# Adding the local attention mask on VectorE, in the pass that finds the row maximum, instead of with a TensorE product

## The chip, the cores and the metric

The kernel runs on one core of one Trainium2 chip. Each core has five engines with queues of their own: TensorE (PE in the profile; its weight loads are listed apart as PEld), VectorE (DVE), ScalarE (ACT), GpSimd (POOL) and SyncE (SP), which here only issues DMA transfers. Matrix products are written to PSUM, a small memory[...]; everything else on the chip lives in SBUF. The metric is the time of one execution on the device in microseconds (us); lower is better.

## The reference

For four sequences of 1024 tokens with 512 features, the reference computes a layer norm, then an attention block and a small matrix product, and adds both to the input. The attention has 16 heads of width 128 and two parts with the same queries. The *sparse* part scores each query against one compressed entry for every 4 tokens, keeps the top 8 and takes a softmax over them. The *local* part scores each query against the keys of its own window of 128 tokens and of the window before, with a band mask:

```
rel = i + WIN - j                       # i: query in window, j: key in the two windows
band = (rel >= 0) & (rel <= WIN)
sl = einsum('bhcqd,bhckd->bhcqk', qc, kw) * scale
sl = where(mask, sl, -1e30)             # mask: band, and no keys before the sequence
pl = softmax(sl)
ctx_local = einsum('bhcqk,bhckd->bhcqd', pl, vw)
merged = (ctx_sparse + ctx_local) * 0.5 # then times Wo
```

The mask of the local part is what the change is about. The first window of a sequence has no window before it, so only 128 keys take part there; all other windows have 256.

## The kernel before

**Tiling.** A *chunk* is 128 tokens of one sequence (number t, 32 in all; c = t mod 8 is its place in the sequence). A *unit* is one pair of heads of one chunk (number n, 256 in all; u = n mod 8 is the pair). Units of one chunk follow each other, u from 0 to 7.

**Pipeline.** The loop at L746 writes the order of all work by hand, and each engine executes its own instructions in that order; the instructions of different engines meet through semaphores, which are inserted from the data that they share. Step s does for several units at once: `scores(s)` for both heads (PE), `keep_context(s-2)` (ACT), `weigh(s)` for both heads (DVE, ACT), `queries(s+2)` (PE), `settle(s)` (DVE), the squares for unit s+2 (ACT, POOL), `settle_window(s)` (ACT), `to_output(s-2)` (PE), `turn(s)` (DVE, then SP), `values_of(s+1)` (PE), `normalize(s+2)` (DVE, POOL), `values(s-1)` (PE), `fetch(s)` (SP), `turn_keys(s+2)` and `fetch_keys(s+2)` (DVE, then SP), and `keep_values(s+1)` (ACT). Between these, two coroutines are advanced a little: `chunk_prep` (layer norm and compressed entries for the chunk after next) and `chunk_eight` (the small product with rounded operands, L422 its last DVE step). In the step with u = 1, `to_output` finishes a chunk, and DVE adds the product to the input (L716).

**The round trip of the keys.** `normalize` scales and rotates the queries and keys of unit s+2; `turn_keys` transposes them in blocks of 32 on DVE (L478, L481) and writes them to a buffer in DRAM (L486); `fetch_keys` reads them back transposed into qT and lkT (L497, L498). Two steps later `scores` uses them. In the same way `turn` (L623) sends the probabilities to DRAM (L631) and `fetch` brings them back (L657). All these transfers are issued by SP in program order, so the keys of unit s+2 are queued behind the probabilities of unit s.

**Scores and their mask.** `scores` fills one PSUM bank per head, sc (two such buffers). Its columns are: 0 to 127 the keys of the window before (absent when c = 0), 128 to 255 those of the own window, and from 256 on (c+1)*32 compressed entries. `loc` names the first group (256 columns, or 128 when c = 0), `spa` the second. In the kernel before, PE writes a mask first, as a product of an identity matrix with the mask in bf16 (L540), and then adds the scores to it in PSUM (L542 for the window before, L549 for the own). The compressed entries come next (L552), and the causal mask of their last 32 columns is added as another product with the identity (L553). A product of fp32 operands is executed as two passes, each with its own weight load; it counts as two instructions in the profile. A bf16 product is one pass.

**The softmax's first step.** `weigh` takes the negated maximum of the local columns (L574, DVE), the top eight of the compressed ones (L575), their negated maximum (L577) and marks them (L578); then ACT exponentiates the local columns (L579, with their sum) and the compressed ones (L582) out of the same bank.

Of the kernel before, what the change touches and what calls it, by code (L numbers as in the profile page):

```python
# [15 lines left out]
AF = mybir.ActivationFunctionType  # L16
ALU = mybir.AluOpType
AX = mybir.AxisListType

P = 128  # L20
# [4 lines left out]
BLK = 32  # L25
# [5 lines left out]
TAKEN = 3e38  # L31
# [7 lines left out]
def kernel(  # L39
# [26 lines left out]
    nc = tc.nc  # L66
# [14 lines left out]
    def blocks(v):  # L81

        return v.rearrange("p (b i) -> p b i", i=BLK)
# [89 lines left out]
    ident_b = const.tile([P, P], BF16, name="ident_b")  # L173
# [4 lines left out]
    mask_b = const.tile([P, 2 * P + NE], BF16, name="mask_b")  # L178
# [249 lines left out]
    def place(n):  # L428

        return divmod(n, NU)  # L430
# [94 lines left out]
    def columns(n):  # L525
        t, _ = place(n)
        c = t % NCH
        lo = 0 if c else P
        m = (c + 1) * NE
        return c, m, ds(lo, 2 * P - lo), ds(2 * P, m)  # L530

    def scores(n, h):
        t, _ = place(n)
        c, m, loc, spa = columns(n)
        w = units[n]
        qT, lkT = w["qT"], w["lkT"]
        ckT, _ = entries[t // NCH]
        sc = psum.tile([P, 512], F32, tag="sc", name=f"sc_{n}_{h}")
        q = qT[:, :, h]
        nc.tensor.matmul(sc[:, loc], ident_b, mask_b[:, loc], start=True, stop=False)  # L540
        if c:
            nc.tensor.matmul(  # L542
                blocks(sc[:, 0:P]),
                q,
                units[n - NU]["lkT"][:, :, ds(h * BLK, BLK)],
                start=False,
                stop=False,
            )
        nc.tensor.matmul(  # L549
            blocks(sc[:, P : 2 * P]), q, lkT[:, :, ds(h * BLK, BLK)], start=False, stop=True  # L550
        )
        nc.tensor.matmul(sc[:, spa], q, ckT[:, 0:m], start=True, stop=False)  # L552
        nc.tensor.matmul(  # L553
            sc[:, ds(2 * P + m - NE, NE)],
            ident_b,
            mask_b[:, 2 * P : 2 * P + NE],
            start=False,
            stop=True,
        )
        heads[n, h] = {"sc": sc}  # L560

    def weigh(n, h):
        c, m, loc, spa = columns(n)
        w = heads[n, h]
        sc = w.pop("sc")
        top = work.tile([P, 8], F32, tag="top", name=f"top_{n}_{h}")
        neg = work.tile([P, 2], F32, tag="neg", name=f"neg_{n}_{h}")
        tot = work.tile([P, 2], F32, tag="tot", name=f"tot_{n}_{h}", bufs=3)
        taken = work.tile([P, 2 * P], BF16, tag="taken", name=f"taken_{n}_{h}")
        prob = probs[h]  # L570
        if n % (NU * NCH) == 0:

            nc.gpsimd.memset(prob[:, 2 * P + NE : 4 * P], 0.0)
        nc.vector.reduce_max(neg[:, 0:1], sc[:, loc], AX.X, negate=True)  # L574
        nc.vector.max(top, sc[:, spa])  # L575

        nc.vector.tensor_scalar(neg[:, 1:2], top[:, 0:1], -1.0, 1e29, ALU.mult, ALU.min)  # L577
        nc.vector.match_replace(taken[:, 0:m], top, sc[:, spa], TAKEN)  # L578
        nc.scalar.activation(  # L579
            prob[:, loc], sc[:, loc], AF.Exp, bias=neg[:, 0:1], accum_out=tot[:, 0:1]  # L580
        )
        nc.scalar.activation(prob[:, spa], sc[:, spa], AF.Exp, bias=neg[:, 1:2])  # L582
        w.update(tot=tot, taken=taken, prob=prob)
# [162 lines left out]
    for s in range(-2, NN + 2):  # L746
# [6 lines left out]
        if u == 3 and 0 <= t and t + 2 < NT:  # L753
            load_x(t + 2)

        for_unit(s, (scores, 0), (scores, 1))
        for_unit(s - 2, (keep_context,))
        for_unit(s, (weigh, 0), (weigh, 1))
        for_unit(s + 2, (queries,))
        for_unit(s, (settle, 0), (settle, 1))  # L760
# [86 lines left out]
```

## Time and profile before

| | |
|---|---|
| median of 3 runs | 2910.0 us (2906.97 to 2914.53) |
| the profiled execution | 2908.4 us, of which 2906.6 us from its first to its last instruction (the span) |
| busy, share of the span | PE 98%, DVE 77%, ACT 44%, POOL 28% |
| one unit, on average | 2906.6 / 256 = 11.4 us |
| L540, mask product | 448 of 128x256 at 271 ns and 64 of 128x128 at 220 ns, PE |
| L574, maximum | 448 over 256 columns at 404 ns and 64 over 128 columns at 271 ns, DVE |

PE's passes overlap in the profile: a pass is listed from the time when it enters the array to its modelled end, so that the mean duration is longer than the distance to the next one. What a pass costs PE is that distance. The chain of waits, which lists the pieces of work that ended last in order of time, gives it directly: each piece there lasts until the next begins. On DVE too, an instruction that waits for nothing may begin before the end of the one before it is listed.

### The profile page before, as it was taken

The numbers are of one execution on the slowest core, as the hardware profiler recorded it, in microseconds if no ns is written. First come the engines' busy times: TensorE is split into PE (matmuls) and PEld (weight loads), VectorE is DVE, ScalarE is ACT, GpSimd is POOL, SyncE is SP. The second block draws the span as 40 slices with busy tenths as digits, with TensorE's granted clock in tenths as the row PEclk, the third lists the DMA queues.
The fourth block names the chain that finished last, engine by engine and source line by source line (L and its number), as shares of the span: only waits on it lengthen the run. The fifth ranks groups of instructions, "written<-read, shape, count | busy, mean of one in ns | idle before, by whom it ended". The sixth has DMA issues, their size and how long they took to land.

```text
span 2906.6 us, 49295 instructions
## 1 busy us (share of the span) xinstructions
PE 2855.3 (98%) x13705; PEld 1899.8 (65%) x13705; DVE 2224.0 (77%) x8636; ACT 1291.5 (44%) x5059; POOL 815.1 (28%) x1126
## 2 busy tenths in 40 slices
PE   5999999999999999999999999999999999999998
PEld 3566666666666666766666666666666666666666
DVE  5777777878777777788877777787887777877776
ACT  2444444444444444444444444444444444444443
POOL 3422222222233222222222332222322323222221
PEclk8999999999999999999999999999999999999999
DMA  8544445554444445454444444554454444455444
GB/s 242 162 129 132 130 134 141 145 146 140 128 115 131 127 130 140 143 144 140 142 126 119 127 130 126 146 148 137 141 143 117 128 124 126 126 146 149 139 142 120
DMA packets 634825, 399.86 MB, mean 138 GB/s; under 512 B 315796, under 2 KB 591030, under 8 KB 634550
## 3 DMA queue, kind: packets, MB, share of 16 engines
q1 hardware_dynamic: 622560, 383.18, 47.2%
q10 hardware_dynamic: 11990, 13.53, 1.5%
q8 instruction: 109, 1.79, 0.3%
q14 instruction: 166, 1.36, 0.2%
HBM read 208.30 MB, written 188.22 MB: 136 GB/s over the span
## 4 chain that ended last, share of the span: by engine, by line
PE 93%; DMA 3%; DVE 1%; SPq 1%; issue 0%; ACT 0%; POOL 0%; ACTq 0%; DVEq 0%; POOLq 0%
PE qp L437 30%; PE op L707 15%; PE vp L506 14%; PE cp L674 13%; PE sc L552 5%; PE sc L549 4%; PE sc L542 4%; PE ep L371 2%; PE qp L438 2%; PE sc L540 2%; DMA lkT<-qk 1%; PE lp L329 1%; PE fp L417 1%; DMA qk<-thb 1%; PE xp L319 0%
## 5 line engine op out<-in xcount | busy, mean ns | idle before, releaser
L437 PE MATMUL qp<-wqk,xnT 128*128 128x512 f32 x2048 | 947.1, 605 | 0.2 <-DMA wqk<-in_L_attn_Wlk_dram 0.2
L437 PEld LDWEIGHTS qp<-wqk,xnT 128*128 128x128 f32 x2048 | 371.3, 191 | 381.2 <-issue 371.0
L579 ACT ACTIVATE prob<-sc,neg 128x256 f32<-128x256 f32 (+1 forms) x512 | 235.6, 460 | 649.8 <-DVE taken L578 639.3
L707 PE MATMUL op<-wo,cT 128*128 128x512 f32 x1024 | 494.4, 605 | 1.0 <-ACT cT L689 1.0
L506 PEld LDWEIGHTS vp<-wlv,xnT 128*128 128x128 f32 x2048 | 388.9, 190 | 161.2 <-issue 103.1
L506 PE MATMUL vp<-wlv,xnT 128*128 128x256 f32 x2048 | 484.0, 379 | 0.0
L623 DVE STREAM_TRANSPOSE probB<-prob 128x512 f32<-128x512 f32 (+2 forms) x510 | 288.7, 603 | 161.1 <-ACT prob L605 157.8
L273 ACT ACTIVATE junk<-qp 128x128 bf16<-128x128 f32 x1024 | 283.6, 277 | 236.5 <-PE qp L438 200.8
L267 POOL TENSOR_SCALAR r<-ss 128x4 f32<-128x4 f32 x256 | 49.8, 194 | 1093.5 <-ACT junk L273 1088.1
L518 ACT COPY lv<-vp 128x256 f32<-128x256 f32 x256 | 95.1, 372 | 537.3 <-PE cp L674 455.1
L286 POOL TENSOR_TENSOR rb<-th,cs 128x256 f32<-128x256 f32 x256 | 247.1, 965 | 286.8 <-DVE th L459 286.8
L459 DVE SCALAR_TENSOR_TENSOR th<-qp,r,norm_w 128x128 f32<-128x128 f32 x1024 | 283.1, 337 | 40.1 <-POOL r L268 40.1
L674 PE MATMUL cp<-probT,lv 128*128 128x128 f32 x1920 | 297.7, 275 | 5.8 <-DMA qk<-thb 3.1
L707 PEld LDWEIGHTS op<-wo,cT 128*128 128x128 f32 x1024 | 181.7, 189 | 174.3 <-issue 96.6
L674 PEld LDWEIGHTS cp<-probT,lv 128*128 128x128 f32 x1920 | 274.8, 191 | 21.1 <-issue 3.6
L268 POOL TENSOR_TENSOR r<-r,nhalf 128x4 f32<-128x4 f32 x256 | 259.7, 1014 | 21.3
L674 PE MATMUL cp<-probT,cv 128*128 128x128 f32 x1536 | 255.2, 275 | 0.0
L574 DVE TENSOR_REDUCE neg<-sc 128x1 f32<-128x256 f32 (+1 forms) x512 | 198.3, 387 | 52.8 <-PE sc L553 52.8
L549 PE MATMUL sc<-lkT,qT 128*128 128x128 f32 x1024 | 210.6, 288 | 27.3 <-DMA lkT<-qk 27.1
L552 PE MATMUL sc<-ckT,qT 128*128 128x96 f32 (+7 forms) x1024 | 226.9, 303 | 0.0
L605 ACT ACTIVATE prob<-prob,tot 128x256 f32<-128x256 f32 (+1 forms) x512 | 222.6, 483 | 3.6 <-DVE tot L599 3.6
L674 PEld LDWEIGHTS cp<-probT,cv 128*128 128x128 f32 x1536 | 212.7, 192 | 0.0
(121 smaller groups left out, 4073.5 us busy)
## 6 DMA issues: line engine op xcount, KB each, us to landing
qk<-thb SPq DMA_DIRECT2D x1024, 64.0 KB, 2.0
pr<-probB SPq DMA_DIRECT2D x127, 512.0 KB, 2.6
probT<-pr SPq DMA_DIRECT2D x508, 128.0 KB, 2.9
pr<-probB SPq DMA_DIRECT2D x96, 384.0 KB, 2.3
probT<-pr SPq DMA_DIRECT2D x384, 96.0 KB, 2.4
qT<-qk SPq DMA_DIRECT2D x256, 128.0 KB, 2.3
lkT<-qk SPq DMA_DIRECT2D x256, 128.0 KB, 2.5
x<-_attn_hidden_states_dram SPq DMA_DIRECT2D x32, 256.0 KB, 3.1
```

The lines of the kernel that those rows point to most:

```text
L268: nc.gpsimd.tensor_tensor(r, r, nhalf[: ss.shape[0], 0:n], ALU.pow)
L273: nc.scalar.activation(junk[: src.shape[0]], src, AF.Square, accum_out=acc)
L286: nc.gpsimd.tensor_tensor(bb, x12, wide(cs[:, HALF:ROPE]), ALU.mult)
L437: nc.tensor.matmul(qp, xnT[:, k, :], wqk_sb[u][:, k, :], start=(k == 0), stop=False)
L459: nc.vector.scalar_tensor_tensor(th[:, i, :], qp[:, ts(i, D)], r[:, i : i + 1], norm_w[:, i // 2, :], ALU.mult, ALU.mult,)
L506: nc.tensor.matmul(vp[:, 0:256], xnT[:, k, :], wlv_sb[u][:, k, :], start=(k == 0), stop=(k == KK - 1),)
L549: nc.tensor.matmul(blocks(sc[:, P : 2 * P]), q, lkT[:, :, ds(h * BLK, BLK)], start=False, stop=True)
L552: nc.tensor.matmul(sc[:, spa], q, ckT[:, 0:m], start=True, stop=False)
L579: nc.scalar.activation(prob[:, loc], sc[:, loc], AF.Exp, bias=neg[:, 0:1], accum_out=tot[:, 0:1])
L623: nc.vector.transpose(pb[:, :, ds(h * g, g), :], prob[:, parts[0] * P : (parts[-1] + 1) * P].rearrange("p (g b i) -> p b g i", b=NB, i=BLK),)
L674: nc.tensor.matmul(blocks(cp[:, h, :]), v, probT[:, :, h * len(parts) + i - parts[0], :], start=(i == parts[0]), stop=(i == parts[-1]),)
L707: nc.tensor.matmul(op, cT[:, h, :], wo_sb[u][:, h, :], start=(u == 0 and h == 0), stop=(u == NU - 1 and h == 1),)
```

## The change

The mask product of the local columns is gone from `scores`; the first product into each group of columns now starts that group. In `weigh`, L574's maximum is replaced by one VectorE instruction that adds the mask to the local scores, multiplies by -1, writes the result back into the same columns of PSUM, and gives its minimum, which is the negated maximum of the masked scores. ACT's exponential then takes these columns with a factor of -1. The mask product of the compressed columns (L553) stays. The instruction issues two on DVE's queue: the pass itself and a read of the accumulator into neg; and as it writes sc, the next one on DVE, the top eight (L575 before), now waits for it.

```diff
         q = qT[:, :, h]
-        nc.tensor.matmul(sc[:, loc], ident_b, mask_b[:, loc], start=True, stop=False)
         if c:
             nc.tensor.matmul(
                 blocks(sc[:, 0:P]),
                 q,
                 units[n - NU]["lkT"][:, :, ds(h * BLK, BLK)],
-                start=False,
-                stop=False,
+                start=True,
+                stop=True,
             )
         nc.tensor.matmul(
-            blocks(sc[:, P : 2 * P]), q, lkT[:, :, ds(h * BLK, BLK)], start=False, stop=True
+            blocks(sc[:, P : 2 * P]), q, lkT[:, :, ds(h * BLK, BLK)], start=True, stop=True
         )
...
-        nc.vector.reduce_max(neg[:, 0:1], sc[:, loc], AX.X, negate=True)
+
+        nc.vector.tensor_tensor_reduce(
+            sc[:, loc], sc[:, loc], mask_b[:, loc], -1.0, TAKEN, ALU.add, ALU.min, neg[:, 0:1]
+        )
         nc.vector.max(top, sc[:, spa])
...
         nc.scalar.activation(
-            prob[:, loc], sc[:, loc], AF.Exp, bias=neg[:, 0:1], accum_out=tot[:, 0:1]
+            prob[:, loc],
+            sc[:, loc],
+            AF.Exp,
+            bias=neg[:, 0:1],
+            scale=-1.0,
+            accum_out=tot[:, 0:1],
         )
```

## The prediction

> **What bounds the kernel now.** I read the page's first and fourth part, then the chain of waits in order of time inside single units, then what DVE waits for inside one chunk, and last DVE's timeline.
>
> ```profile
> PE 2855.3 (98%) x13705; PEld 1899.8 (65%) x13705; DVE 2224.0 (77%) x8636; ACT 1291.5 (44%) x5059; POOL 815.1 (28%) x1126
> PE 93%; DMA 3%; DVE 1%; SPq 1%; issue 0%; ACT 0%; POOL 0%; ACTq 0%; DVEq 0%; POOLq 0%
> ```
>
> PE is 98% busy and carries 93% of the chain, so a pass taken from PE shortens the kernel if nothing else is late. How much a pass costs stands in the chain, in a unit with 256 local columns:
>
> ```profile
> 1559.99 0.11 PE cp L674
> 1560.11 0.11 PE sc L540
> 1560.21 0.24 PE sc L542 x2
> ...
> 1560.87 0.02 PE sc L553
> 1560.89 0.12 PE sc L540
> 1561.01 0.24 PE sc L542 x2
> ...
> 1561.66 0.02 PE sc L553
> 1561.67 3.53 PE qp L437 x8
> ...
> 1565.86 1.72 PE op L707 x4
> ```
>
> L540 takes 0.11 us for head 0 and 0.12 for head 1, though its row in the list of groups says 271 ns: 448 such products are 51 us, 64 shorter ones 4. But the last lines warn. Eight passes of L437 take 3.53 us where four equal passes of L707 take 1.72, so eight should take 3.44. The 0.09 us too many is the first weight load of L437: it stands behind L553, a 32-column product of 0.02 us, which is too short to hide it. After the change L542 of head 1 stands in just that place.
>
> In the chunks with c = 0 the mask product is half as long and hides only half a load:
>
> ```profile
> 820.08 0.02 PE sc L553
> 820.10 0.07 PE sc L540
> 820.16 0.29 PE sc L549 x2
> ```
>
> L549's two passes take 0.29 here and 0.23 to 0.24 behind a full pass.
>
> DVE is the other side. What it waits for in the last chunk of the second sequence, from 1385.1 to 1479.1 us (94.0 us, the widest scores, DVE's tightest stage):
>
> ```profile
> DVE th L288 <- POOL rb L286: 5.0, 8, 0.6
> DVE probB L623 <- ACT prob L605: 3.0, 3, 1.9
> DVE x L716 <- PE op L707: 2.8, 1, 2.8
> DVE neg L574 <- PE sc L553: 1.5, 2, 1.1
> DVE th L459 <- POOL r L268: 1.1, 2, 0.9
> DVE f L422 <- PE fp L417: 0.7, 1, 0.7
> ```
>
> The first line is inside DVE's own chain. The other five lead back to PE (L623 and L459 by way of ACT's squares, which wait for the queries): 9.1 us in eight units, DVE's spare time. The same five come to 12.8 us in the chunk from 848.0 to 934.3 us. DVE is thus behind PE, but not far from binding.
>
> The path by which a late DVE stops PE is the round trip of the keys. PE's largest wait is there:
>
> ```profile
> PE sc L549 <- DMA lkT<-qk: 27.1, 12, 9.1
> ```
>
> About 21 us of it are in the first 130 us. The others sit at one place: units 3 and 4 of a chunk, above all with c = 0. The keys of unit 3 leave DVE in unit 1 just behind L716, which had to wait for PE. In the other chunks these keys land up to about half a us before L549 needs them. So here there is hardly any slack, while the keys of most other units land 1 to 3 us early.
>
> **What the skill says.** The Trainium skill, "TensorE: Matmul & The Clock Gate", section on LDWEIGHTS, prices a load of 128 columns at 128/1.2 = 107 ns; the trace agrees, with 0.09 us exposed behind a product of 0.02 us. "VectorE: DVE Perf Modes", in the section on two Vector instructions with no wait between them, says that an operation which writes out its accumulator is two instructions; the trace shows it at L589, with a read of 82 ns. The same page's tier table puts a two-tensor operation with a PSUM operand at one element per cycle, and its errata section gives (N+151)/0.96 ns for an fp32 sum: an estimate of 424 ns for 256 columns. The trace has 688 ns at 512 columns (L716, one operand in PSUM), where that formula gives 691. No page prices a pass that writes PSUM, and no row of the trace shows one on DVE.
>
> **PE's part.** Head 0 of each unit: L542 follows a full pass of L674, which hides its load, so the whole L540 goes: 0.11 us. Head 1: L542 follows L553; of L540's 0.12 us, 0.09 comes back as exposed load: 0.03 us. That is 0.14 us for each of 224 units, 31 us. For the 32 units with c = 0: head 0 saves 0.06 (L540) and 0.05 (the load it half exposed), head 1 0.07 less 0.04 (0.09 exposed instead of 0.05): again 0.14, together 4.5. PE: 36 us less. The identity's weight loads under L540 (51 us of PEld) vanish with it; they already overlapped.
>
> **DVE's part.** I take the timeline of one unit:
>
> ```profile
> 1330.56 0.38 DVE L589 SCALAR_TENSOR_TENSOR prob<-taken,prob 128x224 f32<-128x224 bf16 x1
> 1330.86 0.08 DVE L589 DVE_READ_ACCUMULATOR prob<-taken,prob 128x1 f32 x1
> 1330.98 0.17 DVE L598 TENSOR_SCALAR tot<-tot 128x2 f32<-128x2 f32 x1
> ...
> 1341.93 0.41 DVE L574 TENSOR_REDUCE neg<-sc 128x1 f32<-128x256 f32 x1
> 1342.27 0.39 DVE L575 MAX8 top<-sc 128x8 f32<-128x224 f32 x1
> ```
>
> Now the maximum is followed by L575 after 0.34 us (0.31 to 0.34): L575 waits for nothing and starts under L574's tail. The new pass has the shape of L589: two streams, an accumulator, then an instruction that waits for it. There the distance from start to dependent start is 0.42 us at 224 columns; 32 more columns at 34 ns (420 against 386 ns in the rows) give 0.46. So +0.13 us per head, and the same at 128 columns (by the same distances there, 0.22 + 0.12 against 0.20): 512 x 0.13 = 67 us more on DVE, 0.26 us per unit. The bounds of the unknown: below, the pass cannot spare the read and the wait, 0.12; above, PSUM read and written in one bank at half rate adds 256 cycles' worth, 0.27 more, hence 0.40. I take 0.13, the nearest row.
>
> **The rest.** ACT's exponentials start 0.13 and 0.26 us later; ACT sits idle 650 us before them in all, and what is queued behind them, the squares, waits for the queries anyway (201 us). With that cover gone it would cost the same 0.26 per unit. The factor -1 is in the same instruction. POOL and SP issue nothing more or less; no DMA changes.
>
> **What comes back.** In a chunk with c > 0 DVE needs 16 x 0.13 = 2.1 us more and PE 1.1 less, 3.2 out of 9.1 to 12.8 us spare: PE stays the bound on average. But the key waits grow. Keys of unit 3: between the end of PE's output product in unit 1 and their use, DVE gains nothing (no `weigh` lies between), while PE arrives 0.14 + 0.11 = 0.25 us sooner; with slack between 0 and 0.5 I take 0.17 us, 28 chunks, 5 us. Keys of unit 4: one unit of DVE lies between (0.26) and PE comes 0.39 sooner; slack was mostly 0.5 to 2, so 0.1 us, 3 us. With c = 0 the waits at units 3 and 4 exist already: there DVE sets the pace from unit 1 to 4, and three chunks lose about 0.6 us each, 2 us. The start-up (units 0 to 4, DVE-paced) and the last units, where weighing lies on the final chain, cost two to four times 0.26 together: 2 us. In sum 12 us returned.
>
> 36 - 12 = 24 us: span 2906.6 to 2883, the profiled execution 2908.4 to 2884, and against the median of 2910.0, 2886 us. A measurement of this kernel tells about 0.3% (9 us) from no change.
>
> **Rivals.** *The full saving*: the loads hide after all (they might be fetched while L552 runs) and key waits don't grow: 51 + 4 = 55 us, 2855. L437 behind L553 speaks against it. *The wait takes the gain*: the new pass costs towards 0.40 per head. The keys of unit 4 then come 0.8 later on DVE's side with PE 0.4 sooner, so that a slack of 1 is gone, and those of unit 5 lose 1.6 and 0.5 of their 2 to 3. About 0.5 to 1 us per chunk more is lost, 16 to 32 us: 2902 to 2918, no change. L716's agreement with the price of plain streaming speaks against it. *VectorE becomes the bound, slower*: the pass has a large fixed cost, being of a kind that no row shows. With 9.1 to 12.8, on average about 10.7 us spare per chunk and 16 heads, DVE reaches today's period at 10.7/16 = 0.67 us more per head, so at 1.0 us from the pass to the top eight; each 0.1 us above costs 51 us, and at 1.1 us it is 2961.
>
> **Chances.** My forecast (2874 to 2896) 0.58; the full saving or near it (below 2874) 0.12; the eaten gain (2897 to 2918) 0.17, a sixth of it still over 0.3% faster; the slower case 0.13. Hence faster 0.73, same 0.14, slower 0.13. The range 2862 to 2916 holds the first case, half of the second and nearly all the third.
>
> **What would show it.** Right: L542's first pass takes about 0.20 us in head 1 and 0.12 in head 0; the new pass shows some 420 to 500 ns and an accumulator row of about 80 ns, the top eight starting 0.46 us after it; DVE's five PE-bound waits in the last chunk fall from 9.1 to about 6; lkT waits rise from 27 to 35 or 40 us. Wrong: the pass takes 0.7 us or more, PE's busy share falls visibly below 98% with lkT or qT waits spread over all units, or head 1 shows no exposed load.

## The result and the profile after

The changed kernel takes **2886.7 us** (median of four runs, 2879.2 to 2890.4) against 2911.0 us of the kernel before on the same chip (2907.0 to 2914.5). The ratio is 0.9914, with a 95% interval of 0.9890 to 0.9937: 24 us or 0.9% faster. The profiled execution took 2890.4 us with a span of 2888.6 us; it happens to be the slowest of the four, and where that matters a second profile of the same kernel stands beside it.

The names of the lines have moved by the edit. L541, L548, L551 and L552 are the old L542, L549, L552 and L553 (scores of the window before, of the own window, of the compressed entries, and their mask); L574 is the new pass, L577 the top eight (was L575), L612 ACT's scaling of the local probabilities (was L605), which stands behind the squares of unit s+2 (L273) in ACT's order, L630 and L723 the old L623 and L716, L681 the product with the probabilities (was L674).

The page's first part, busy time with its share of the span and the number of instructions:

```profile
PE 2828.1 (98%) x13193; PEld 1872.0 (65%) x13193; DVE 2298.1 (80%) x9148; ACT 1286.2 (45%) x5059; POOL 815.7 (28%) x1126
```

PE has lost its 512 mask products (13705 to 13193) and is still busy 98% of a shorter span. DVE has gained 512 instructions, the reads of the accumulator, and 74 us of busy time.

**What a unit saves on PE.** PE's timeline has this in a unit of the last chunk of the second sequence. Columns: start, listed duration, line, operation, tiles, operand shapes, count.

```profile
1387.89 0.40 PE L541 MATMUL sc<-lkT,qT 128*128 128x128 f32 x2
1388.13 0.40 PE L548 MATMUL sc<-lkT,qT 128*128 128x128 f32 x2
1388.36 0.60 PE L551 MATMUL sc<-ckT,qT 128*128 128x256 f32 x2
1388.80 0.18 PE L552 MATMUL sc<-mask_b,ident_b 128*128 128x32 bf16 x1
1388.83 0.48 PE L541 MATMUL sc<-lkT,qT 128*128 128x128 f32 x2
1389.15 0.40 PE L548 MATMUL sc<-lkT,qT 128*128 128x128 f32 x2
```

Read the distances from start to start. L541 of head 0 holds PE for 1388.13 - 1387.89 = 0.24 us, as before. L541 of head 1, which now stands behind the 32-column product L552, holds it for 1389.15 - 1388.83 = 0.32 us. The 0.08 us too many is, by the prediction's account, the weight load that nothing hides; experiment 6 tests that. The rows of the list of groups, with shapes kept apart, say the same. Before (busy time, mean ns of one, idle time ahead and what ended it):

```profile
L542 PE MATMUL sc<-lkT,qT 128*128 128x128 f32 x896 | 178.8, 281 | 1.1 <-DMA qT<-qk 1.1
```

The same row after:

```profile
L541 PE MATMUL sc<-lkT,qT 128*128 128x128 f32 x896 | 197.3, 302 | 3.3 <-DMA qT<-qk 2.1 <-ACT cT L696 1.0
```

A unit has four such passes. A mean that is 21 ns longer is one pass in four that is 0.08 us longer.

The distance from one unit's small mask products to the next unit's is the period of a unit. Unit by unit, after less before, its median is -0.136 us; 256 times that is 34.8 us. What is missing from 34.8 to the change of the span came back at single units. The table gives the excess over the median, in us, for both profiles of the changed kernel:

| | this profile | second profile | predicted |
|---|---|---|---|
| span, after less before | -18.0 | -24.8 | -24 |
| 256 x the median unit | -34.8 | -34.8 | -36 |
| first chunk of all and last chunk of all | +5.6 and +2.6 | +1.1 and +1.3 | +2 |
| other chunks with c = 0 | +1.9 | -1.0 | +2 |
| c > 0: from unit 2 to unit 3 | +4.7 | +4.3 | +5 |
| c > 0: from unit 3 to unit 4 | +0.4 | +2.3 | +3 |
| the rest | +1.7 | +2.0 | 0 |

Not all of this is waiting. In the first 130 us TensorE is granted only part of its clock, and not the same part in every execution. The rows give, for the 40 us from 40 to 80 us, PE's busy time, the granted clock as a share of full speed, the DMA share and GB/s: before, then this profile, then the second.

```profile
40.00:80.00 40.00, 30.20 (x127) 0.84 0.68 205
40.00:80.00 40.00, 28.06 (x96) 0.73 0.62 186
40.00:80.00 40.00, 30.77 (x120) 0.82 0.70 208
```

In this profile the clock is lower there, and the step from unit 1 to unit 2 alone is 3.1 us over the median; in the second profile, with nearly the clock of before, it is 0.6 us under it. This profile also has a stretch with a granted clock of 0.62 (1501.5 to 1506 us, in the first chunk of the third sequence, after a wait of 2.0 us for keys), and the unit there is 1.5 us over. So some 5 of its 16.8 us go with the clock (an estimate from these two places); the second profile's 10.0 us are the better measure of what the waits took. Over all executions on record the same shows: at a granted clock of 0.993, 0.994 and 0.995 the changed kernel has medians of 2889, 2884 and 2879 us (six, two and one executions), the kernel before 2913, 2911 and 2909 (six, 26 and 19), so that at like clock the gain is 24 to 30 us. Whether the change itself lowers the clock is not shown.

**What a head costs on DVE.** DVE's timeline of one head:

```profile
1344.18 0.40 DVE L574 CUSTOM_DVE_ANT_0 sc<-sc,mask_b 128x256 f32<-128x256 f32 x1
1344.50 0.14 DVE L574 DVE_READ_ACCUMULATOR2_ANT neg<- 128x1 f32 x1
1344.67 0.40 DVE L577 MAX8 top<-sc 128x8 f32<-128x224 f32 x1
```

From the pass to the top eight it is 0.49 us here; the median over the heads with 256 columns is 0.51, against 0.33 before. So a head costs DVE 0.18 us more, 92 us in all. The pass alone is only 10 ns longer than the maximum it replaces (414 ns against 404). What is new is the read of the accumulator, and that the top eight starts only after it:

```profile
L574 DVE CUSTOM_DVE_ANT_0 sc<-sc,mask_b 128x256 f32<-128x256 f32 x448 | 185.3, 414 | 10.8 <-PE sc L552 9.1
L574 DVE DVE_READ_ACCUMULATOR2_ANT neg<- 128x1 f32 x512 | 70.9, 138 | 0.0
```

**Who waits for whom.** The waits of DVE in the last chunk of the second sequence, 1375 to 1468 us (sum, count, longest):

```profile
DVE th L288 <- POOL rb L286: 5.0, 8, 0.6
DVE x L723 <- PE op L714: 2.2, 1, 2.2
DVE probB L630 <- ACT prob L612: 1.8, 3, 0.6
DVE th L459 <- POOL r L268: 1.4, 2, 1.1
```

Of the five waits that lead back to PE, two are gone, and the others come to 2.2 + 1.8 + 1.4 = 5.4 us where they were 9.1. PE's waits for the transfers, over the whole span:

```profile
PE sc L548 <- DMA lkT<-qk: 29.7, 12, 9.2
PE cp L681 <- DMA probT<-pr: 8.8, 4, 3.8
```

The keys' wait has grown by 2.6 us only (27.1 before), and the probabilities' by 6.2 (2.6 before).

### The profile page after: what moved, and what is told of

Read it like the earlier page. It is cut to its first block, busy times and chain, and to the rows that moved or that the text cites. A ratio compares the mean times of both kernels' runs of the same rounds, so it can differ in the third digit from the quotient of the medians.

```text
span 2888.6 us, 49258 instructions
## 1 busy us (share of the span) xinstructions
PE 2828.1 (98%) x13193; PEld 1872.0 (65%) x13193; DVE 2298.1 (80%) x9148; ACT 1286.2 (45%) x5059; POOL 815.7 (28%) x1126
## 5 line engine op out<-in xcount | busy, mean ns | idle before, releaser
L630 DVE STREAM_TRANSPOSE probB<-prob 128x512 f32<-128x512 f32 (+2 forms) x510 | 288.6, 603 | 99.1 <-ACT prob L612 96.2
L273 ACT ACTIVATE junk<-qp 128x128 bf16<-128x128 f32 x1024 | 284.2, 278 | 123.0 <-PE qp L438 95.7
L459 DVE SCALAR_TENSOR_TENSOR th<-qp,r,norm_w 128x128 f32<-128x128 f32 x1024 | 283.0, 337 | 53.6 <-POOL r L268 53.6
L681 PE MATMUL cp<-probT,lv 128*128 128x128 f32 x1920 | 298.2, 275 | 8.8 <-DMA probT<-pr 8.8
L681 PEld LDWEIGHTS cp<-probT,lv 128*128 128x128 f32 x1920 | 275.3, 192 | 24.2 <-issue 6.0
L681 PE MATMUL cp<-probT,cv 128*128 128x128 f32 x1536 | 255.6, 275 | 0.0
L548 PE MATMUL sc<-lkT,qT 128*128 128x128 f32 x1024 | 211.6, 289 | 30.1 <-DMA lkT<-qk 29.7
L551 PE MATMUL sc<-ckT,qT 128*128 128x96 f32 (+7 forms) x1024 | 226.9, 303 | 0.0
L612 ACT ACTIVATE prob<-prob,tot 128x256 f32<-128x256 f32 (+1 forms) x512 | 222.8, 484 | 2.8 <-DVE tot L606 2.8
L574 DVE CUSTOM_DVE_ANT_0 sc<-sc,mask_b 128x256 f32<-128x256 f32 (+1 forms) x512 | 203.4, 397 | 23.0 <-PE sc L552 21.2
L288 DVE TENSOR_TENSOR th<-thb,rb 128x128 f32<-128x128 f32 x256 | 87.2, 341 | 158.5 <-POOL rb L286 158.0
```

The costliest lines, as they stand in the source:

```text
L273: nc.scalar.activation(junk[: src.shape[0]], src, AF.Square, accum_out=acc)
L459: nc.vector.scalar_tensor_tensor(th[:, i, :], qp[:, ts(i, D)], r[:, i : i + 1], norm_w[:, i // 2, :], ALU.mult, ALU.mult,)
L548: nc.tensor.matmul(blocks(sc[:, P : 2 * P]), q, lkT[:, :, ds(h * BLK, BLK)], start=True, stop=True)
L630: nc.vector.transpose(pb[:, :, ds(h * g, g), :], prob[:, parts[0] * P : (parts[-1] + 1) * P].rearrange("p (g b i) -> p b g i", b=NB, i=BLK),)
L681: nc.tensor.matmul(blocks(cp[:, h, :]), v, probT[:, :, h * len(parts) + i - parts[0], :], start=(i == parts[0]), stop=(i == parts[-1]),)
```

## The experiments

Every time is a median, with its range, beside the kernel before on the same chip (2910.0 to 2911.1 us). "Per unit" is the median change of a unit's period against before. The local score columns are called loc, as in the code; lines marked ... leave out code.

**1. PE's part alone.** The local mask is left out altogether: no product, and the plain maximum. Against the changed kernel:

```diff
-        nc.vector.tensor_tensor_reduce(
-            sc[:, loc], sc[:, loc], mask_b[:, loc], -1.0, TAKEN, ALU.add, ALU.min, neg[:, 0:1]
-        )
+        nc.vector.reduce_max(neg[:, 0:1], sc[:, loc], AX.X, negate=True)
...
-            scale=-1.0,
```

> PE's part alone: the mask product of the local columns is taken out and nothing takes its place; VectorE finds the plain maximum as before. (The local scores are left unmasked.) My theory (head 0 saves 0.11 us, head 1 only 0.03, since the weight load of its first pass stands exposed behind the 32-column product): 35 us less PE time, some 4 us of it given back in waits for keys, so about 2879 us, and L437-like 0.20 us for the first pass in head 1. Rival (PE saves the whole 55 us and VectorE's dearer pass gives the other half back): about 2855 us.

Measured: 2880.0 us (2877.1 to 2882.9), ratio 0.9897 (0.9884 to 0.9910), per unit -0.136. So 31 us is what PE's part brings with no cost on DVE at all. The 55 us of the full saving do not exist in this order of work: the passes of L541 have a mean of 302 ns here too. The whole change stands at 2886.7, so DVE's part would cost some 7 us; the two intervals (0.9884 to 0.9910 and 0.9890 to 0.9937) overlap, so this is not told from nothing.

**2. DVE's part alone.** The mask product stays and the new pass is added; the mask is added twice.

```diff
-        nc.vector.reduce_max(neg[:, 0:1], sc[:, loc], AX.X, negate=True)
+        nc.vector.tensor_tensor_reduce(
+            sc[:, loc], sc[:, loc], mask_b[:, loc], -1.0, TAKEN, ALU.add, ALU.min, neg[:, 0:1]
+        )
...
-            prob[:, loc], sc[:, loc], AF.Exp, bias=neg[:, 0:1], accum_out=tot[:, 0:1]
+            prob[:, loc], sc[:, loc], AF.Exp, bias=neg[:, 0:1], scale=-1.0, accum_out=tot[:, 0:1]
```

> VectorE's part alone: the mask product stays on TensorE, and VectorE runs the new pass too (the mask is added twice, which changes nothing in the result). VectorE has 0.18 us more per head, 92 us in all. My theory: it is hidden except in waits for the keys of units 3 and 4 of a chunk, 2 to 8 us, so 2912 to 2918 us. Rival (VectorE's part costs what the change did not gain of 55 us): about 30 us more, 2940 us. If VectorE's time were on the path: 3000 us.

Measured: 2913.4 us (2908.1 to 2917.4), ratio 1.0011 (1.0004 to 1.0017), per unit 0.000. DVE does 92 us more work and the kernel takes 3 us longer. That is the cover at work: the five waits of DVE that the prediction counted as spare (the list of the kernel before is in experiment 4) fall from 389 to 302 us, by nearly as much as was added. Whether the same 92 us cost more when PE is faster at the same time (7 us by experiment 1) can't be told from these times.

**3. One head at a time.** Which head saves what? Both edits were made for one head only, `h == 0` or `h == 1`; the other keeps product and maximum. The edit for head 0:

```diff
+        product = h != 0
+        if product:
+            nc.tensor.matmul(sc[:, loc], ident_b, mask_b[:, loc], start=True, stop=False)
...
-                start=True,
-                stop=True,
+                start=not product,
+                stop=not product,
...
+        fused = h == 0
+        if fused:
+            nc.vector.tensor_tensor_reduce(
...
+        else:
+            nc.vector.reduce_max(neg[:, 0:1], sc[:, loc], AX.X, negate=True)
...
-            scale=-1.0,
+            scale=-1.0 if fused else 1.0,
```

> The change for head 0 of each unit alone; head 1 keeps the mask product and the plain maximum. My theory: head 0's product goes whole, 0.109 us x 256 = 28 us less PE time, VectorE has only half of its extra cost, some 4 us come back as waits: about 2886 us, as good as the whole change. Rival (both heads save the same, VectorE gives back in proportion): half of the change's gain, about 2899 us.

> The change for head 1 of each unit alone; head 0 keeps the mask product and the plain maximum. My theory: the exposed weight load takes 0.08 of the 0.11 us saved, 0.028 us x 256 = 7 us less PE time, some 3 us come back as waits: about 2906 us. Rival (both heads save the same): half of the change's gain, about 2899 us.

| | time, us | ratio | per unit | mean of the 896 L541 passes |
|---|---|---|---|---|
| head 0 | 2895.9 (2893.9 to 2897.6) | 0.9952 (0.9939 to 0.9965) | -0.109 | 282 ns |
| head 1 | 2906.6 (2902.4 to 2912.2) | 0.9991 (0.9983 to 0.9998) | -0.027 | 302 ns |

PE's saving splits just as the prediction had it, 0.11 and 0.03 us, and only head 1 shows the exposed load. The times are another matter. Head 1 fits. Head 0 was expected at 2886 and took ten more: of its 256 x 0.109 = 27.9 us, 13 came back, 8.0 of them on the way into unit 3, in steps of 1 to 2 us in a few chunks. The theory of this run (some 4 us of return) is wrong there. The two heads together gain 14.6 + 3.9 = 18.5 us, against 24 for the whole. Why head 0 alone lost more at unit 3 than the whole change does is left open.

**4. Where does DVE become the bound?** One or two plain maxima, whose result nobody uses, were added per head ahead of the new pass; the edit for one (`range(2)` for two):

```diff
+        for _ in range(1):
+            nc.vector.reduce_max(spare, sc[:, loc], AX.X, negate=True)
         nc.vector.tensor_tensor_reduce(
```

> The changed kernel with two plain maxima more per head on VectorE ahead of the new pass, results unused: 2 x 0.331 us by the distance measured before, so VectorE has 0.18 + 0.66 = 0.84 us per head more than in the kernel before. My theory (spare time of 9 to 13 us per chunk, used up at 0.67 us per head, each 0.1 us above costs 51 us): VectorE sets the pace, about 2911 + 87 = 2998 us, 2980 to 3020. Rival (VectorE is so loosely coupled that only the keys of units 3 and 4 come later): under 2930 us.

> The changed kernel with one plain maximum more per head, result unused: VectorE then has about 0.18 + 0.34 = 0.52 us per head more than in the kernel before. The run with two more stood at 0.97 us and lost 252 us, which with a slope of 512 heads puts the point where VectorE sets the pace of before at 0.97 - 0.49 = 0.48 us, not at the 0.67 of my prediction: the waits behind ScalarE and GpSimd (L623, L459) are no spare time of VectorE's, those behind TensorE alone are (97 + 53 + 41 us and a part of L623's 158). Theory now: 2910 + 0.04 x 512 = 2930 us, 2918 to 2945. The prediction's threshold: 2910 us or less.

| DVE per head against before | time, us | ratio | change |
|---|---|---|---|
| +0.18 us (the change) | 2886.7 | 0.9914 | -24 us |
| +0.52 us (one more) | 2960.7 (2955.5 to 2977.1) | 1.0182 (1.0156 to 1.0208) | +50 us |
| +0.97 us (two more) | 3162.0 (3159.0 to 3163.2) | 1.0862 (1.0847 to 1.0877) | +252 us |

DVE got 0.97 us more with two maxima, not the 0.84 expected: both write the same small tile, so the second waits for the first and starts 0.44 us after it, where one that waits for nothing starts after 0.33. Even so, both times came out far above what was expected; the expectation for one more maximum was already revised after the run with two, and is still 30 us too low. The prediction took 0.67 us per head as the point at which DVE reaches the period of the kernel before. With 0.52 the kernel should have been faster than before, or the same; it is 50 us slower. The page of the kernel with two more shows that PE no longer binds (211 of its PE records are missing from the trace, 12982 against 13193 weight loads, nearly all of them L438 at 0.21 us each, so that the true share is about 93%):

```profile
PE 2911.4 (92%) x12982; PEld 1914.6 (61%) x13193; DVE 2653.3 (84%) x10172; ACT 1238.6 (39%) x5059; POOL 814.6 (26%) x1126
```

But DVE is busy only 84%. What it still waits for says where the count of the spare time went wrong (DVE's waits over the whole span; sum, count, longest):

```profile
DVE th L288 <- POOL rb L286: 157.4, 255, 0.6
DVE probB L633 <- ACT prob L615: 93.0, 122, 4.2
DVE th L459 <- POOL r L268: 61.9, 83, 2.3
DVE spare L576 <- PE sc L552: 14.7, 5, 6.4
DVE x L726 <- PE op L717: 12.0, 5, 6.0
```

And the same view of the kernel before:

```profile
DVE probB L623 <- ACT prob L605: 157.8, 154, 4.6
DVE x L716 <- PE op L707: 97.4, 32, 6.1
DVE neg L574 <- PE sc L553: 52.8, 52, 6.0
DVE f L422 <- PE fp L417: 41.1, 31, 1.9
DVE th L459 <- POOL r L268: 40.1, 83, 2.3
```

The waits that name PE have nearly gone: the output product from 97 to 12 us, the scores from 53 to 15, L422 from 41 to less than one. But the wait for ACT's scaling (L605, L615 here), which stands behind the squares in ACT's order, falls from 158 to 93 only, and the one for POOL, which works on the squares' sums, rises from 40 to 62. The prediction traced these two back to PE, since the squares wait for the queries. With two more maxima that is over: ACT's idle time ahead of the squares, in the rows of before and of this kernel, falls from 236.5 to 37.8 us ("remote" is what the view prints where it can name no releaser).

```profile
L273 ACT ACTIVATE junk<-qp 128x128 bf16<-128x128 f32 x1024 | 283.6, 277 | 236.5 <-PE qp L438 200.8 <-POOL rb_e L286 7.1 <-POOL er L268 2.2
L273 ACT ACTIVATE junk<-qp 128x128 bf16<-128x128 f32 x1024 | 283.3, 277 | 37.8 <-remote 8.8
```

So 155 us of the two waits remain although the squares hardly wait for PE any longer: they were never spare in this order of work. What DVE could give is the difference of the two lists: 85 + 38 + 41 + 65 - 22 = 207 us, or 0.40 us per head, not 0.67. The curve agrees: if all DVE time past the threshold counts in full, 252 us from 512 heads put it at 0.97 - 0.49 = 0.48 us. It has no sharp corner. From +0.18 to +0.52 us per head the time rises by 74 us where 174 were added to DVE, from there to +0.97 by 201 where 230 were added. The loss begins before the average is used up. With one more maximum the median unit is still 0.135 us shorter than before, as in the change; the loss sits in single units, and shows on PE in part as small waits for queries and keys:

```profile
PE sc L548 <- DMA lkT<-qk: 41.3, 31, 9.0
PE sc L541 <- DMA qT<-qk: 18.8, 26, 1.7
```

These two are 28 us more than in the change (29.7 and 2.1), of the 74 us; the rest was not followed. A rival for the loss with two more is TensorE's clock, 0.98 over the whole span where before had 0.995. It is not the cause: two chunks of the same place in their sequence (c = 6), one with a granted clock of 1.00 and one with 0.98, both last 102.0 us, against 93.3 before.

**5. Is the SP queue what makes the keys late?** The keys of unit s+2 are written behind the probabilities of unit s in the same queue. Here the writes of the keys are issued ahead of the fetch of the probabilities. DVE's transposes move with them in the program, but the fetch has no work for DVE, so DVE's own order stays:

```diff
+        for_unit(s + 2, (turn_keys,))
         if s < NN - 1:
             for_unit(s, (fetch,))
...
-        for_unit(s + 2, (turn_keys,), (fetch_keys,))
+        for_unit(s + 2, (fetch_keys,))
```

> The changed kernel with the writes of the keys ahead of the fetch of the probabilities in SP's order; the reads of the keys stay behind it. The keys then leave some 0.5 us sooner, the probabilities land some 2 to 3 us later. If the keys' round trip through SP is what gave back the 10 us (my theory), the waits for lkT beyond the first 130 us (about 8 us in the profile) fall to 2 or less and the time to about 2880 us, provided the probabilities are still in time; if they are not, PE waits at the product with the values instead and the time goes up. Rival (the waits come from VectorE's pass itself): the same 2887 us.

Measured: 2892.4 us (2891.7 to 2896.2), ratio 0.9940 (0.9928 to 0.9953): 5.7 us above the change, though the two intervals touch. PE's waits:

```profile
PE cp L681 <- DMA probT<-pr: 24.6, 38, 4.5
PE sc L548 <- DMA lkT<-qk: 14.5, 5, 9.3
```

After the first 130 us the key waits are down to 1.3 us (7.0 in the change), as the theory of the queue says. But the probabilities are late in their place, 38 times instead of 4. The two round trips share one queue with no slack for either; putting one first moves the wait to the other.

**6. Is the exposed load due to what stands ahead of it?** If so, a long pass ahead of L541 of head 1 must hide it. The mask products of the compressed entries (L552) of both heads were moved behind the scores of both heads, into a function of their own:

```diff
-        nc.tensor.matmul(
-            sc[:, ds(2 * P + m - NE, NE)],
...
+    def end_scores(n):
+        _, m, _, _ = columns(n)
+        for h in range(2):
+            nc.tensor.matmul(
+                heads[n, h]["sc"][:, ds(2 * P + m - NE, NE)],
...
-        for_unit(s, (scores, 0), (scores, 1))
+        for_unit(s, (scores, 0), (scores, 1), (end_scores,))
```

> The changed kernel with the two 32-column mask products of the compressed entries put together behind both heads' other products. Head 1's first product then follows a pass of head 0 with as many columns as there are compressed entries (32 in the first chunk of a sequence, 256 in the last). My theory (a weight load[...] is hidden only as far as the pass before it lasts): the 0.08 us exposed in head 1 is gone in the last chunks (0.08 us per unit less), halved in the middle, unchanged in the first; about 9 us in all, 2878 us, if VectorE's later start on head 0 (by some 0.7 us) costs nothing. Rival (the 0.20 us of the first pass is not an exposed load): no unit gets shorter, 2887 us.

PE's timeline of this kernel; L557 holds the two mask products:

```profile
1380.59 0.60 PE L551 MATMUL sc<-ckT,qT 128*128 128x256 f32 x2
1381.03 0.39 PE L541 MATMUL sc<-lkT,qT 128*128 128x128 f32 x2
1381.26 0.40 PE L548 MATMUL sc<-lkT,qT 128*128 128x128 f32 x2
```

L541 of head 1 now holds PE for 0.23 us, and the mean of its passes is back:

```profile
L541 PE MATMUL sc<-lkT,qT 128*128 128x128 f32 x896 | 181.5, 284 | 6.6 <-DMA qT<-qk 3.8 <-ACT cT L700 2.6
```

The saving per unit grows with the length of the pass ahead, L551, which has 32 columns for c = 0, 64 for c = 1 and so on: -0.14, -0.17, -0.19, -0.22 us for c = 0 to 3, and -0.23 from c = 4 on. That is the exposed load, disappearing as the cover gets longer: L541 of head 1 holds PE for 0.29, 0.26 and 0.24 us at c = 1, 2 and 3 and 0.23 from c = 4 on, where the change has 0.32 throughout. Summed over the places in the sequence, PE's saving is 52 us. The kernel takes 2885.3 us (2879.5 to 2887.0), ratio 0.9910 (0.9892 to 0.9927): not to be told from the change. Its profile's span is 24 us shorter than before's, so that 28 of the 52 us came back, 5.7 of them on the way into unit 3 and most of the others spread over many units. Two causes offer themselves: with DVE 0.18 us per head slower, little cover is left to use a faster PE; and head 0's scores are complete only after head 1's, so that DVE starts on them later. Experiment 8 keeps the second and removes the first.

**7. What makes the pass dear on DVE?** The masked scores were written to SBUF, into prob, where ACT exponentiates them in place. The top eight then does not wait for the pass, which no longer writes the tile (sc, one bank of PSUM) that it reads.

```diff
-            sc[:, loc], sc[:, loc], mask_b[:, loc], -1.0, TAKEN, ALU.add, ALU.min, neg[:, 0:1]
+            prob[:, loc], sc[:, loc], mask_b[:, loc], -1.0, TAKEN, ALU.add, ALU.min, neg[:, 0:1]
...
             prob[:, loc],
-            sc[:, loc],
+            prob[:, loc],
             AF.Exp,
```

> The changed kernel with the masked scores written to SBUF, where the exponential then reads them, instead of back into PSUM. The top eight then need not wait for the pass. Expected: the pass itself 0.42 us as before if writing PSUM costs nothing extra, less if it does; from its start to the top eight 0.40 to 0.48 us instead of 0.51; the time within 5 us of 2887, since VectorE's time is hidden.

DVE's timeline:

```profile
1331.29 0.38 DVE L574 CUSTOM_DVE_ANT_0 prob<-sc,mask_b 128x256 f32<-128x256 f32 x1
1331.61 0.08 DVE L574 DVE_READ_ACCUMULATOR2_ANT neg<- 128x1 f32 x1
1331.61 0.39 DVE L577 MAX8 top<-sc 128x8 f32<-128x224 f32 x1
```

The top eight starts together with the read of the accumulator, 0.32 us after the pass (median 0.34, as before the change). So the 0.18 us per head lies in the order "pass, read, then the top eight", and not in the second operand or the multiplication: the pass takes 403 ns into SBUF, 414 into PSUM, and the plain maximum 404. Two parts of it can be told apart. A wait alone costs 0.11 us, as between the two useless maxima of experiment 4, which write to SBUF (0.44 us against 0.33). Most of the rest, 0.06, is the read, 138 ns in the change and 82 here. L589's read also takes 82 ns, although an instruction waits for it, and its pass writes SBUF; so the output in PSUM is the likelier reason for the longer read than the waiter. But L589 is another instruction, and a pass into PSUM with no waiter behind it was not run. The time is 2883.6 us (2882.5 to 2884.3), ratio 0.9906 (0.9891 to 0.9921). That is 3 us below the change, less than the intervals can tell: the 92 us were nearly all hidden.

**8. Both.** Experiment 6 saves 17 us more on PE, of which nothing shows in the time; experiment 7 gives DVE the time to follow.

> The changed kernel with both edits: the 32-column mask products of the two heads together behind both heads' other products (which took 21 us more from TensorE's passes but only 1 to 2 from the time), and the masked scores written to SBUF (which takes 0.17 us per head from VectorE). Theory: what swallowed the first edit's gain is VectorE, on whose work the keys depend, so that with its relief a good part of the 21 us shows: 2865 to 2876 us. Rival (it is the transfers alone, which the relief does not touch): 2882 us, as with one edit.

> The changed kernel once more, beside the two others on one chip: 2887 us.

| | time, us | ratio to before |
|---|---|---|
| both (6 and 7) | 2873.7 (2871.1 to 2876.8) | 0.9872 (0.9857 to 0.9887) |
| the change, again | 2888.1 (2883.6 to 2892.6) | 0.9922 (0.9909 to 0.9935) |

The page of both (211 PE records are missing here too):

```profile
PE 2793.1 (97%) x12982; PEld 1866.3 (65%) x13193; DVE 2210.6 (77%) x9148; ACT 1349.1 (47%) x5059; POOL 818.8 (28%) x1126
```

This is the fastest version, 37 us below the kernel before. Alone the two edits brought 1 and 3 us over the change, together 13 to 14: of the 52 us that PE saves, 37 now arrive in the time (33 in this profile). Head 0's later start is the same as in experiment 6, so what held experiment 6 back was for the most part DVE's time, not that start and not the transfers alone; 15 us still do not arrive.

## Why the prediction was right

The time (2886 predicted, 2886.7 measured) and the net of 24 us are right, and so is the mechanism: PE binds, part of its saving is lost to an exposed load, and late transfers give some of the rest back. That the two agree within 1 us is luck: DVE's cost was set too low, the places of the return were partly wrong, and the granted clock moves the time by more than that. The steps, one by one:

**PE's saving, 36 us: right.** 34.8 measured. Head 0 0.109 and head 1 0.027 us per unit were shown apart by experiment 3; that head 1 gives so little because of a weight load was shown by experiment 6. The Trainium skill, "TensorE: Matmul & The Clock Gate", section on LDWEIGHTS, has 107 ns for a load of 128 columns. Here the load behind a pass of 0.03 us exposes 0.08, and together that is 0.11, which agrees. The rival of the full saving falls with experiment 1.

**DVE's added time, 0.13 us per head: too low.** It is 0.18, inside the bounds of 0.12 and 0.40. The analog, L589, was right about the kind of cost (a read, and a wait for it) and wrong about its size: the accumulator row is 138 ns instead of 82, the sign of about 80 ns failed, and so did the top eight at 0.46 us. What is missing from 0.13 to 0.18 is about that longer read (experiment 7). The mistake cost little, since the cover held: the whole of DVE's part is worth 3 to 7 us (experiments 1, 2 and 7).

**DVE's waits in the last chunk, from 9.1 to about 6: right,** 5.4.

**What comes back, 12 us: right as a sum, half right in its places.** 16.8 us in the first profile, of which some 5 go with the clock, and 10.0 in the second. The way into unit 3 loses 4.7 and 4.3 us where 5 were predicted. But it isn't 0.17 us in each of 28 chunks: five chunks, the same ones in both profiles, lose 0.7 to 1.5 us each, and most lose next to nothing. The slack at this place is not spread evenly between 0 and 0.5 us. In experiment 3 three other chunks joined with 1.6 to 2.3 us each, and the sum was missed. Unit 4 lost less than predicted in one profile.

**The sign of the keys: failed.** The waits for lkT were to rise to 35 or 40 us and rose to 29.7 (26.1 in the second profile). The step behind it, that late keys alone would give the gain back, is wrong: the probabilities, queued with the keys on SP, took as much (8.8 us against 2.6), and experiment 5 shows that the two trade places. With one more maximum (experiment 4) the key waits do reach 41, so the mechanism is there, at more DVE time.

**VectorE as the bound, from 0.67 us more per head: wrong in its threshold.** This rival didn't come about, but its step was tested, and it failed: the prediction counted as spare all DVE waits but the first of its list, also those that lead to PE "by way of ACT's squares", L623 and L459. Of 198 us in these two, 155 remain when PE no longer binds. The usable spare is 0.40 us per head by the waits and 0.48 by the time, both estimates from the runs of experiment 4; the rival should have started at 0.73 to 0.81 us from the pass to the top eight, not at 1.0. Its price, 51 us for each 0.1 us, holds as an upper end: 45 between the last two kernels, 22 between the change and the first of them.

**The wait takes the gain (0.40 us per head): not what happened,** since the cost was 0.18. Between the change and one more maximum, the line through -24 us at 0.18 and +50 at 0.52 crosses zero near 0.29, so as a mechanism it begins earlier than the prediction had it.

## What to carry to other kernels

A product taken off the bounding TensorE is worth its distance to the next pass, less the weight load that it was hiding: look at the length of what will then stand ahead of the next load, and reorder if it is short (here that alone brought 1 us, and 10 us once VectorE had time to follow). When work goes to another engine, look at which instructions behind it now have to wait for it; here the read and the wait cost 0.18 us per head and the arithmetic 0.01, and another output tile took both away. An engine's waits are spare only if they end when the bounding engine does; waits in a loop with a third engine stay, and a run with some useless work added shows how much is left.

## What was not expected of the hardware

A VectorE pass that reads and writes the same columns of a PSUM bank and reads a second operand from SBUF costs 414 ns for 256 columns, against 404 for the plain maximum and 403 for the same pass into SBUF: in the pass itself, reading and writing the one bank costs next to nothing. The read of the accumulator behind it takes 138 ns instead of 82.

What costs is the wait between two VectorE instructions. The top eight starts 0.34 us after a pass of 0.40 us when it is independent, and 0.51 us after it when it has to wait for it and its read; a plain maximum starts 0.33 or 0.44 us after another. The Trainium skill, "VectorE: DVE Perf Modes", says in "The DRAIN you can't avoid" that a semaphore between chained copies "costs nothing extra", and adds that a next operation that isn't held starts earlier. The second statement is what these traces show; the first doesn't hold here, where a wait between two maxima costs 0.11 us.

Weight loads hide in degrees. In experiment 6 the exposed part shrinks by some 0.03 us with each 32 columns of the fp32 product ahead (0.29, 0.26 and 0.24 us for the two passes behind 64, 96 and 128 columns), and is gone at 160 (0.23).
